# A Mamba scan's decay, states and sums in rings of their own, with one score tile fewer

## The chip, the cores and the metric

The kernel runs on one core of a Trainium2 chip. The metric is the device time of one execution, in microseconds (us), as the median of three runs. TensorE (PE in the profile, with its weight loads as PEld), VectorE (DVE), ScalarE (ACT), GpSimd (POOL) and SyncE (SP, which issues the DMAs) each work through a queue of their own in order. An instruction whose input is not ready holds up everything behind it on its engine.

## The reference

The model has two layers on eight batch rows of 64 latent tokens (width 512), which read a context of 1601 tokens per batch row. Everything is float32.

```
x = x + xattn0(layernorm(x), ctx)    # 32 query heads, 8 key/value heads of 128, over 1601 context rows
x = x + mamba(layernorm(x))          # d_in 1024, 16 states
x = x + ffn0(layernorm(x))           # ternary weight
x = x + xattn1(layernorm(x), ctx)    # softmax(x ctx^T) ctx
x = x + attn1(layernorm(x))          # causal, 32 heads
x = x + ffn1(layernorm(x))           # ternary octonion weights, gated
```

The part that the change touches is the recurrence inside `mamba`:

```
dA    = exp(dt_t * A)                          # decay, per channel and state
state = state * dA + (dt_t * u_t) * B_t        # over 64 time steps
y     = sum over the 16 states of state * C_t
```

after which `y + u * D` is gated and multiplied by the output matrix.

## The kernel before

The work is two programs that share the engines. The large one, `x_all`, is the first cross attention. It goes through 64 units, one for each batch row and key/value head. A unit has six steps. In these, PE projects keys (`x_k`, line 363) and values (`x_v`, line 334) from the context, makes scores of 13 blocks of 128 context rows (`x_s`, line 385), and multiplies the exponentials of the unit before by its values (`x_av`, line 464). ACT and DVE take the results out of PSUM: ACT copies values (line 337) and scores (line 388), and splits keys into a high and a low part with DVE (lines 108 and 109). DVE keeps the running maximum (lines 390, 392, 395), subtracts it (line 426) and normalises (lines 476, 477, 479). POOL sums the exponentials (lines 429, 446, 448, 452). Four PSUM buffers (`KVB = 4`) are shared by keys, values and scores.

The scores of a unit take seven tiles `S` of 128x512. They are written in one unit and read in the next, by the exponential, by POOL's sum and by PE's product with the values (`AVPLAN`: the product begins in the third step of the next unit). The ring of `S` holds `SB` tiles, 11 before the change. So the first four tiles of the new unit find a place at once, and each later one has to wait until a tile of the old unit has been read for the last time.

The second program is made of side chains: first a preparation of weights (`prep`), then for every pair of batch rows a `chain` of the other five blocks. While `x_all` runs, it reports a cost after each piece of its work, and `advance` lets each chain go forward as far as the constants `SPAN`, `CHAIN_COST` and `X_COST` say. The chains of the first three pairs run beside `x_all`; the chain of the fourth runs after it, with a path and buffers of its own (`tail`), together with what is left of the third. On DVE, ACT and POOL every instruction of a chain is pinned behind whatever was recorded before it on its engine (class `Late`). The instructions of `x_all` are not pinned: a scheduler that plays the program through on a model of the chip places them, and it may put later ones ahead of a pinned instruction that is not ready in its model. So the size of a ring changes the order of all the queues.

Beside `x_all`, `mamba` does its recurrence in 32 pieces per pair, eight blocks of 128 channels for each of four groups of four states (`scan`, line 895). A piece works on two tiles of 128x512, the decay `da` and the states `h`:

1. ACT: four exponentials into `da`; POOL: a memset of the first column of `da`, in some pieces `du = dt * u`, and then `h = B * du`.
2. DVE: the scan, which reads `da` and `h` and writes `h`.
3. `h * C`, on DVE in even pieces and on POOL in odd ones.
4. DVE: the sum over the states into `y`, and the addition to `u`.

`y` is the first quarter of `da`, so `da` is in use until the end of the piece. Both come from the ring `a2` of the pool for Mamba. One of its five tiles is held throughout by the transposed input of the block, which the gates after the scan still read, so four are left for the scan: two pieces. `a2` also serves the weights of the projections (`tw`: W_in, W_x and W_dt, loaded at lines 816, 844 and 869), the temporaries of `silu` and `softplus` (three at a time), the gate `z` and the split of the output (`mamba_out`). `B` and `C` come by a DMA (line 889) into `bc`, which has one buffer, once for each group of states: four times per pair.

Of the kernel before, what the change touches and what calls it, by code (L numbers as in the profile page):

```python
# [16 lines left out]
P = 128  # L17
D = 512
NC = 4
T = 64  # L20
# [16 lines left out]
PINNED = ("vector", "scalar", "gpsimd")  # L37
WOB = 3
KVB, OB, MB = 4, 1, 1
VB, SB = 16, 11  # L40
VPLAN = ((), (0,), (1, 2), (3,), (4, 5), (6,), (7,), (8,), (9, 10), (11,), (12,), ())
KPLAN = (1, 2, None, 3, None, 0)
CPLAN = (0, 1, 2, None, None, 3)
AVPLAN = ((), (), (0, 1, 2, 3), (4, 5, 6, 7), (8, 9, 10, 11), (12,))
EXPLAN = ((0,), (1, 2), (3,), (4, 5), (6,), ())
BUFS = {"a2": 5, "lv": 3, "bc": 1, "xpad": 1, "b2": 5, "b4": 2, "w2": 3, "xr": 2}
BUFS_TAIL = {"a2": 6, "du": 2, "bc": 2, "xpad": 4, "s4": 11, "kb": 3, "b2": 8, "b4": 3, "w2": 12, "xr": 2}


# [29 lines left out]
class Kernel:  # L79
# [13 lines left out]
    def sb(self, tag, shape, dt=FP, bufs=None, pool=None):  # L93
        if pool is None:
            pool, bufs = self.ca if tag in MAMBA_TAGS else self.cp, bufs or self.bufs.get(tag)
            if tag in REST and self.tp and not self.tail:
# [710 lines left out]
    def mamba(self, gi, x, xo):  # L807
# [40 lines left out]
        sm = self.sb("sm", [64, P], bufs=1)  # L848
# [36 lines left out]
        def bcast(sh):  # L885
            bc = self.sb("bc", [P, 2, HS, 2, T])
            for a in range(2):
                r = a * NST + sh * HS
                nc.sync.dma_start(
                    out=bc[:, a].rearrange("p s b t -> p (s b t)"),  # L890
                    in_=self.bc_s[gi][r : r + HS].rearrange("r t -> (r t)")[None, :].to_broadcast([P, HS * P]),
                )
            return bc

        def scan(c, sh, bc):
            da = self.sb(self.td, [P, HS, 2, T])
            for s in range(HS):
                k = sh * HS + s
                nc.scalar.activation(da[:, s], dt[:, c], AF.Exp, scale=self.A[:, c, k : k + 1])
            nc.gpsimd.memset(da[:, :, :, 0:1], 0.0)  # L900
            du = dus[:, c]
            if sh == 0:
                nc.gpsimd.tensor_tensor(du, dt[:, c], u[:, c], ALU.mult)
            h = self.sb(self.ts, [P, HS, 2, T])
            nc.gpsimd.tensor_tensor(h, bc[:, 0], du[:, None].to_broadcast([P, HS, 2, T]), ALU.mult)

            yield 1
            hf, df = h.rearrange("p s b t -> p (s b t)"), da.rearrange("p s b t -> p (s b t)")
            nc.vector.tensor_tensor_scan(hf, df, hf, 0.0, ALU.mult, ALU.add)
            yield 1  # L910
            (nc.gpsimd if c % 2 else nc.vector).tensor_tensor(h, h, bc[:, 1], ALU.mult)
            yield 1
            y = da[:, 0]
            nc.vector.tensor_reduce(y.rearrange("p b t -> p (b t)"), h.rearrange("p s b t -> p (b t) s"), AX.X, ALU.add)
            nc.vector.scalar_tensor_tensor(u[:, c], u[:, c], self.Dp[:, c : c + 1] if sh == 0 else 1.0, y, ALU.mult, ALU.add)
            yield 1

        wps = None
        if tail:
# [18 lines left out]
            for c in range(NCH):  # L938
                du = self.sb("du", [P, 2, T])
                nc.gpsimd.tensor_tensor(du, dt[:, c], u[:, c], ALU.mult)  # L940
                for k0 in range(0, NST, CS):
                    da = das[k0 // CS % 2]
                    for s in range(CS):
                        nc.scalar.activation(da[:, s, :, 1:], dt[:, c, :, 1:], AF.Exp, scale=self.A[:, c, k0 + s : k0 + s + 1])
                    bc, o = bcs[k0 // HS], k0 % HS
# [17 lines left out]
        else:  # L963
            for sh in range(nh):
                bc = bcast(sh)
                for c in range(NCH):
                    yield from scan(c, sh, bc)
# [332 lines left out]
    def run(self):  # L1300
        nc, tc, ctx = self.nc, self.tc, self.ctx
        nc.scalar.preload_act_table_set("natural_log_exp_and_others")
        self.setup(bufs=BUFS, accb=2, hs=4, tail=False, ahead=1, **TAGS)
        self.pc = ctx.enter_context(tc.tile_pool(name="pc", bufs=2, space=PSUM))
# [68 lines left out]
            advance(now)  # L1373


TAGS = {"tw": "a2", "ts": "a2", "td": "a2", "tc4": "b4", "tk": "b2", "t4": "w2", "tl": "b2", "tn": "w2", "tv": "lv"}
TAGS_TAIL = {"tw": "w2", "ts": "s4", "td": "s4", "tc4": "s4", "tk": "kb", "t4": "s4", "tl": "s4", "tn": "w2", "tv": "s4"}
ENV = ("nc", "cp", "ca", "pc", "bufs", "accb", "hs", "tail", "ahead", *TAGS)
GROUPS = {8: [2, 2, 2, 2], 2: [2]}
SPAN = [3.1,3.1,2.6,0.2]  # L1380
PREP_END = 2.8
MAMBA_TAGS = ("a2", "lv", "bc", "xpad", "sm")
FFN_TAIL = (("l", 0), ("l", 1), ("a", 0), ("l", 2), ("a", 1), ("d", 0), ("a", 2), ("d", 1), ("d", 2))
REST = {"w2":8,"b4":3}
OTB = 1
# [114 lines left out]
```

## Time and profile before

| | us |
|---|---|
| median of three runs | 2729.16 (2728.2 to 2729.43) |
| profiled execution, its own time | 2721.08 |
| its span | 2719.3 |
| PE busy | 2565.7 |
| DVE busy | 1746.8 |
| ACT busy | 1352.6 |
| POOL busy | 1171.4 |
| first to last scan, first pair | 768.5 to 1040.7 |
| first to last scan, second pair | 1411.3 to 1690.9 |
| first to last scan, third pair | 2033.3 to 2308.1 |

The span is from the first to the last instruction, 1.8 us less than the execution's own time. The profiled execution is 8.1 us shorter than the median of the runs. A row of the view by stretches gives a window, its length, and for each engine the busy time in it with the number of instructions, then the granted clock of PE as a share of full speed, the share of the DMA engines that were busy, and GB/s. In a row of the timeline the first number is the start, the second the duration, and the bracket at the end tells how long the engine had been idle and what ended that.

### The profile page before, as it was taken

What the parts mean: (1) busy time and instruction counts of PE and PEld (TensorE: products, weight loads), DVE (VectorE), ACT (ScalarE), POOL (GpSimd) and SP (SyncE); (2) the same over time, 40 slices, a digit from 0 to 9 for tenths busy, and PEclk for the clock granted to TensorE, in tenths of its full rate; (3) what the DMA queues carried; (4) which work ended last, traced back from release to release, by engine and by line L of the source; (5) the groups of instructions that cost most, each with busy time, mean ns of one, the idle gap of its engine ahead of it and who ended that gap; (6) DMA issues with size and microseconds to landing.
All of it is one profiled execution on the core that took longest, in us unless ns stands there. A gap on an engine that the chain in (4) does not pass through costs nothing.

```text
span 2719.3 us, 43920 instructions
## 1 busy us (share of the span) xinstructions
PE 2565.7 (94%) x16288; PEld 2273.7 (84%) x16288; DVE 1746.8 (64%) x2843; ACT 1352.6 (50%) x3128; POOL 1171.4 (43%) x1123
## 2 busy tenths in 40 slices
PE   7999999999998899999999988999999998986888
PEld 6999999889887899978988987997897898964644
DVE  4544345577688886545568689544668879457854
ACT  4444554445565554544455554544555455445543
POOL 3212434464588643422357346421249445114610
PEclk9999999999999999999999998999999999997999
DMA  9544446665665234665234443565342463476575
GB/s 308 153 141 153 138 144 228 200 204 178 214 218 188 75 121 159 211 184 174 88 109 134 152 136 106 185 206 186 116 133 80 128 187 113 148 256 201 195 264 188
DMA packets 302934, 455.59 MB, mean 168 GB/s; under 512 B 80248, under 2 KB 179576, under 8 KB 298240
## 3 DMA queue, kind: packets, MB, share of 16 engines
q1 hardware_dynamic: 302720, 452.79, 52.2%
q8 instruction: 128, 2.10, 0.3%
q14 instruction: 86, 0.70, 0.1%
HBM read 380.23 MB, written 72.48 MB: 166 GB/s over the span
## 4 chain that ended last, share of the span: by engine, by line
PE 47%; DVE 11%; DMA 4%; POOL 3%; issue 3%; ACT 2%; POOLq 0%; DVEq 0%; ACTq 0%; SPq 0%
PE v_ps L334 10%; PE k_ps L363 10%; PE o_ps L464 6%; PE s_ps L385 5%; DVE a L65 4%; PE w_ps L521 2%; PE acc L819 2%; PE acc L777 2%; PE acc L774 1%; PE acc L1092 1%; PE acc L1036 1%; POOL a L65 1%; POOL ss L452 1%; DVE acc L953 1%; PE acc L1178 1%
## 5 line engine op out<-in xcount | busy, mean ns | idle before, releaser
L363 PE MATMUL k_ps<-cxb,wk 128*128 128x384 f32 x2304 | 473.5, 348 | 36.4 <-DVE kt L109 12.6
L334 PE MATMUL v_ps<-wv,cxb 128*128 128x256 f32 x3456 | 474.1, 283 | 7.4 <-DVE mx L392 3.9
L334 PEld LDWEIGHTS v_ps<-wv,cxb 128*128 128x128 f32 x3456 | 441.8, 190 | 28.9 <-issue 13.6
L363 PEld LDWEIGHTS k_ps<-cxb,wk 128*128 128x128 f32 x2304 | 406.8, 192 | 56.3 <-DVE kt L109 14.3
L385 PE MATMUL s_ps<-q,kt 128*128 128x256 f32 (+1 forms) x2496 | 414.5, 299 | 8.6 <-DVE mx L392 7.2
L464 PE MATMUL o_ps<-S,v 128*128 128x256 f32 (+1 forms) x1664 | 413.6, 381 | 2.6 <-DVE rw L479 1.7
L388 ACT COPY S<-s_ps 128x512 f32<-128x512 f32 (+1 forms) x448 | 242.5, 554 | 252.6 <-PE s_ps L385 249.0
L385 PEld LDWEIGHTS s_ps<-q,kt 128*128 128x128 f32 (+1 forms) x2496 | 342.0, 185 | 30.3 <-DVE mx L392 8.5
L392 DVE TENSOR_TENSOR mx<-s_ps,mx 128x512 f32<-128x512 f32 x256 | 175.4, 685 | 297.5 <-ACT S L388 297.2
L452 POOL TENSOR_TENSOR ss<-ss,S 128x512 f32<-128x512 f32 x254 | 356.6, 1404 | 14.9 <-ACT S L427 0.3
L429 POOL TENSOR_TENSOR ss<-S,S 128x512 f32<-128x512 f32 x64 | 84.0, 1312 | 640.0 <-ACT S L427 639.9
L464 PEld LDWEIGHTS o_ps<-S,v 128*128 128x128 f32 (+1 forms) x1664 | 299.4, 190 | 41.6 <-issue 5.6
L426 DVE TENSOR_TENSOR S<-S,m_ps 128x512 f32<-128x512 f32 (+1 forms) x448 | 257.5, 641 | 36.2 <-PE m_ps L412 35.4
L108 ACT ACTIVATE kt<-k_ps,c_bk 128x384 fp32r<-128x384 f32 (+1 forms) x256 | 151.8, 593 | 246.2 <-PE k_ps L363 245.4
L427 ACT ACTIVATE S<-S 128x512 f32<-128x512 f32 (+1 forms) x448 | 247.6, 600 | 41.4 <-DVE S L426 41.0
L109 DVE SCALAR_TENSOR_TENSOR kt<-k_ps,c_bk,kt 128x384 fp32r<-128x384 f32 (+1 forms) x256 | 160.9, 629 | 156.2 <-ACT kt L108 155.0
L337 ACT COPY v<-v_ps 128x256 f32<-128x256 f32 (+1 forms) x416 | 152.1, 368 | 195.8 <-PE v_ps L334 192.7
L334 PE MATMUL v_ps<-wv,cxt 128*128 128x256 f32 (+1 forms) x1536 | 211.3, 286 | 5.1 <-DVE mx L392 5.1
L334 PEld LDWEIGHTS v_ps<-wv,cxt 128*128 128x128 f32 (+1 forms) x1536 | 194.6, 176 | 17.3 <-issue 5.9
L363 PE MATMUL k_ps<-cxt,wk 128*128 128x450 f32 x768 | 179.3, 376 | 0.0
L65 DVE TENSOR_TENSOR_SCAN a<-a,a 128x512 f32<-128x512 f32 x96 | 153.9, 1603 | 32.2 <-POOL a L65 32.0
L65 ACT ACTIVATE a<-lv,c_A_log 128x128 f32<-128x128 f32 x384 | 122.8, 392 | 85.8 <-DVE a L65 84.8
(358 smaller groups left out, 3951.3 us busy)
## 6 DMA issues: line engine op xcount, KB each, us to landing
wo<-d_wo SPq DMA_DIRECT2D x96, 512.0 KB, 5.6
wk<-d_wk SPq DMA_DIRECT2D x63, 512.0 KB, 4.3
wv<-d_wv SPq DMA_DIRECT2D x31, 1024.0 KB, 5.7
cst<-in_ctxT_dram SPq DMA_DIRECT2D x96, 192.0 KB, 2.7
b<-in_ctxN_dram SPq DMA_DIRECT2D x36, 512.0 KB, 3.8
d_q<-q_t SPq DMA_DIRECT2D x32, 512.0 KB, 4.3
q<-d_q SPq DMA_DIRECT2D x64, 256.0 KB, 3.0
d_wo<-b SPq DMA_DIRECT2D x32, 512.0 KB, 2.9
```

The costliest lines, as they stand in the source:

```text
L65: return lambda *a, **k: self.tc.keep_in_program_order(f(*a, **k))
L109: eng.scalar_tensor_tensor(lo, src, bias, hi.bitcast(FP), ALU.add, ALU.subtract)
L334: nc.tensor.matmul(ps[:r], lhsT=cx[:, a, c, o : o + r], rhs=w[:, m, c, :], start=k == 0, stop=k == 11)
L337: nc.scalar.copy(vt[:r], ps[:r])
L363: nc.tensor.matmul(ps[:, :wd], lhsT=w[:, a, c, :], rhs=cx[:, m, c, :], start=k == 0, stop=k == 11)
L385: nc.tensor.matmul(sp[:r, gi, :], lhsT=kt[:, a, o : o + r], rhs=q[:, m, :], start=k == 0, stop=k == 2)
L388: nc.scalar.copy(s[:r, :n], sp[:r, :n])
L392: nc.vector.tensor_tensor(mx, sp, S[0] if len(S) == 1 else mx, ALU.max)
L426: nc.vector.tensor_tensor(sv, sv, ps[:r, 1:2].to_broadcast([r, w, 256]), ALU.add)
L427: nc.scalar.activation(sv, sv, AF.Exp, scale=ISC)
L452: nc.gpsimd.tensor_tensor(ss, ss, S[n], ALU.add)
L464: nc.tensor.matmul(ps[:, 0], lhsT=self.v[(b, j, t)][:r, hc : hc + P], rhs=S[t // 2][:r, t % 2], start=t == 0, stop=t == NT - 1)
```

## The change

The decay `da` gets a ring `d` of two tiles, the sums `y` a ring of two small tiles (128x128) in place of a quarter of `da`, and the states share `a2`, which goes from five tiles to four. The scores `S` go from eleven tiles to ten. Per partition the decay takes 4 KB and the sums 1 KB, while `a2` and `S` give back 2 KB each. No instruction is added or removed. The path of the last pair (`BUFS_TAIL`, `TAGS_TAIL`) is as before.

```diff
-VB, SB = 16, 11
+VB, SB = 16, 10
...
-BUFS = {"a2": 5, "lv": 3, "bc": 1, "xpad": 1, "b2": 5, "b4": 2, "w2": 3, "xr": 2}
+BUFS = {"d": 2, "a2": 4, "y": 2, "lv": 3, "bc": 1, "xpad": 1, "b2": 5, "b4": 2, "w2": 3, "xr": 2}
...
-            y = da[:, 0]
+            y = self.sb("y", [P, 2, T])
             nc.vector.tensor_reduce(y.rearrange("p b t -> p (b t)"), h.rearrange("p s b t -> p (b t) s"), AX.X, ALU.add)
...
-TAGS = {"tw": "a2", "ts": "a2", "td": "a2", "tc4": "b4", "tk": "b2", "t4": "w2", "tl": "b2", "tn": "w2", "tv": "lv"}
+TAGS = {"tw": "a2", "ts": "a2", "td": "d", "tc4": "b4", "tk": "b2", "t4": "w2", "tl": "b2", "tn": "w2", "tv": "lv"}
...
-MAMBA_TAGS = ("a2", "lv", "bc", "xpad", "sm")
+MAMBA_TAGS = ("d", "a2", "y", "lv", "bc", "xpad", "sm")
```

## The prediction

> **What bounds the kernel now.** I read the page's engine totals first, then its groups, then the windows around the scans, then the timeline at single stalls.
>
> ```profile
> PE 2565.7 (94%) x16288; PEld 2273.7 (84%) x16288; DVE 1746.8 (64%) x2843; ACT 1352.6 (50%) x3128; POOL 1171.4 (43%) x1123
> ```
>
> PE is the bound, idle for 2719.3 - 2565.7 = 153.6 us. A change that leaves PE's work alone can only win or lose there. The next view cuts each of the three scan stages into four quarters of eight pieces, by the start of every eighth scan. The first number behind the length is PE's busy time, the third DVE's.
>
> ```profile
> core 0: us, PE busy (x) PEld busy (x) DVE busy (x) ACT busy (x) POOL busy (x), PEclk, DMA share, GB/s
> 768.50:844.70 76.20, 67.79 (x425) 63.93 (x425) 67.44 (x76) 42.67 (x101) 64.47 (x60) 0.93 0.67 224
> 844.70:921.70 77.00, 63.78 (x407) 60.24 (x405) 66.04 (x75) 45.68 (x115) 59.90 (x57) 0.96 0.42 124
> 921.70:984.60 62.90, 61.12 (x411) 58.75 (x411) 51.52 (x76) 33.83 (x83) 34.99 (x34) 1.00 0.31 94
> 984.60:1045.00 60.40, 60.40 (x398) 57.57 (x397) 50.11 (x74) 32.53 (x81) 33.67 (x32) 1.00 0.40 127
> 1411.30:1530.00 118.70, 115.07 (x796) 104.77 (x796) 91.90 (x136) 67.16 (x160) 78.58 (x74) 1.00 0.37 110
> 1530.00:1613.10 83.10, 82.74 (x527) 77.56 (x526) 61.29 (x90) 43.04 (x104) 34.64 (x38) 1.00 0.54 172
> 1613.10:1657.40 44.30, 36.94 (x215) 34.28 (x215) 40.07 (x53) 21.94 (x59) 25.54 (x29) 0.88 0.36 121
> 1657.40:1693.00 35.60, 26.73 (x151) 23.94 (x150) 34.88 (x45) 17.78 (x48) 18.46 (x19) 0.86 0.28 85
> 2033.30:2113.00 79.70, 76.70 (x524) 65.24 (x523) 70.43 (x96) 48.18 (x121) 71.80 (x70) 1.00 0.31 89
> 2113.00:2209.70 96.70, 92.27 (x572) 84.97 (x571) 71.92 (x106) 47.75 (x117) 42.97 (x44) 0.98 0.46 141
> 2209.70:2271.90 62.20, 59.79 (x384) 55.89 (x382) 51.38 (x79) 34.51 (x86) 32.61 (x32) 1.00 0.55 166
> 2271.90:2313.00 41.10, 35.04 (x216) 31.87 (x216) 38.18 (x53) 19.82 (x53) 24.33 (x25) 0.96 0.34 108
> ```
>
> PE's idle time is 8.4, 13.2, 1.8 and 0 us in the first pair, 3.6, 0.4, 7.4 and 8.9 in the second, 3.0, 4.4, 2.4 and 6.1 in the third: 59.6 us. It follows DVE's share. At 74 to 88% PE loses 0 to 4.4 us; in the three short quarters, at 90 to 98%, it loses 6 to 9. The first pair's two early quarters (88 and 86%) lose 8 and 13, since the preparation of weights loads POOL and DVE there too. Where PE idles, DVE sets the pace.
>
> ```profile
> L65 DVE TENSOR_TENSOR_SCAN a<-a,a 128x512 f32<-128x512 f32 x96 | 153.9, 1603 | 32.2 <-POOL a L65 32.0
> L65 ACT ACTIVATE a<-lv,c_A_log 128x128 f32<-128x128 f32 x384 | 122.8, 392 | 85.8 <-DVE a L65 84.8
> ```
>
> The ring shows here. ACT waits 84.8 us for DVE before exponentials (the decay waits for the sum of the piece two before it). But the scan's own 32.0 us of waiting is for POOL's `h`, much of it where `bc` had just been loaded.
>
> **The ring of decay and states.** Decay of piece c+2 now waits for scan c in place of its sum; `h` of piece c+2 no longer waits for the end of piece c. Nothing is added: 96 sums write another tile at the same 1068 ns. What does it free? This is the longest such wait but one:
>
> ```profile
> 1655.10 0.58 ACT L388 COPY S<-s_ps 128x512 f32<-128x512 f32 x1
> 1662.52 1.28 ACT L65 ACTIVATE a<-lv,c_A_log 128x128 f32<-128x128 f32 x4 [6.84 <-DVE a L65]
> 1663.70 0.56 ACT L108 ACTIVATE kt<-k_ps,c_bk 128x384 fp32r<-128x384 f32 x1
> ...
> 1657.36 2.34 DVE L65 TENSOR_TENSOR_SCAN a<-a,a 128x512 f32<-128x512 f32 x1 [3.22 <-POOL a L65]
> 1662.40 0.69 DVE L392 TENSOR_TENSOR mx<-s_ps,mx 128x512 f32<-128x512 f32 x1
> ```
>
> ACT is idle for 6.84 us with a key split behind it. PE then stands for 4.49 us, but it waits for the maximum at 1662.40, and DVE had worked without a break from 1657.36. Freed ACT finds the same DVE queue. Directly recoverable is the stall that ACT itself ends (scores after a copied value, 0.9 us) and part of PE's 4.5 us for the split output: I take -1, between 0 and -5.
>
> The Trainium skill (Perfetto Trace Analysis, Optimization Strategy) says that one gap repeating on the engine that should be saturated can mean too little memory for the next tile. Here it repeats on ACT, half idle; by the rule alone the ring would be worth up to the 84.8 us, by the row -1.
>
> Built, the change leaves more DVE work between an odd scan and its sum, which waits for POOL's product: at most two instructions stand there in 10 of 48 pieces, where it was 21. DVE waits 21.9 us for POOL before these sums. Half would go, and only DVE-bound quarters pass it on: -3, between 0 and -11.
>
> **Crowding.** The queue order of the built kernel shows how many of the cross attention's own DVE instructions stand in each quarter. Before: 47, 46, 48, 46; 76, 50, 24, 23; 45, 54, 43, 24. After: 62, 28, 48, 46; 68, 51, 23, 14; 46, 66, 28, 21. The side chain advances faster against the main work and clumps. Such a row takes DVE about 0.65 us (its maxima 0.685, splits 0.629, subtractions 0.641), and stands for 26.73 / 23 = 1.2 to 36.94 / 24 = 1.5 us of PE. In a DVE-bound quarter every row fewer thus adds 0.5 to 0.9 us of idle PE; I use 0.7. Second pair: 1 and 9 rows fewer, +7. Third pair: 3 rows, +2; and 43 to 28 goes four fifths of the way from a loss of 2.4 to one of 6.1, +3. First pair: the first quarter falls from 8.4 to the roomy quarters' 4, -4; the second loses 18 rows, +13, of which half, since it starts from 86% and PE can run ahead: +6. Roomy quarters: -1. Together +13. Four PSUM buffers let PE run some 4 x 1.5 us ahead at each clump, so I take half: +7, between 0 and +17 (all of it, and a third more).
>
> The clock is lower there too: 0.86 to 0.88 where PE idles most. The scan lasts 1.17 us at least but 1.60 on average, and 21 of the 96 last over 2.1, mostly 2.3, with a POOL product beside them. The Trainium skill (SBUF, Who interferes with whom) says DVE with two SBUF inputs and a reading POOL instruction exclude each other for the whole instruction. The trace agrees: 2.3 is about 1.2 plus a POOL product's 1.3. By the rule a denser stage could add 1.3 us to each of the 75 scans that are shorter than 2.1 us, up to 98 us of DVE; by the row the mean stays, and nothing is added here.
>
> **Ten score tiles.** From the score copies, POOL's sums and the value products I worked out when each tile is last read. With eleven the ring bites twice, 1.0 and 0.3 us:
>
> ```profile
> 806.41 0.59 ACT L388 COPY S<-s_ps 128x512 f32<-128x512 f32 x1 [0.99 <-PE o_ps L464]
> ```
>
> With ten at the same times, six of 448 copies would come too early, by 9.9, 5.6, 1.2, 0.8, 0.8 and 0.7 us, all in scan stages. Behind a waiting copy stand ACT's value and key evictions, so the PSUM buffers, so PE. The built order moves the value products of the worst unit ahead of its fourth score pair, which removes the 9.9. I take +3, between 0 and +19.
>
> **The narrower `a2`.** Three free tiles in place of four outside the scan. `softplus` takes three, so W_dt's second half loads only when one is given back; gates share two tiles for weights and `silu`. PE waited once for such a load (3.1 us; W_dt takes 2.6 to 5.3 to land). Three pairs: +3, between 0 and 3 x 4.0 = +12. SP's queue behind the load holds weights of the cross attention, ordered around it.
>
> **The tail.** In the built order two more of the third chain's eight score accumulations stand before the end of the main work. Each cost 4.5 to 5.8 us in the tail (3.4 to 4.7 of load, 1.1 of PE), and puts about 2 us of PE into the main part: -2, between -9 and +4.
>
> **Sum:** -1 - 3 + 7 + 3 + 3 - 2 = +7. The profiled execution's 2721.1 becomes 2728. It lies 8.1 below the median of the runs; on the median 2729.2 + 7 = 2736 us.
>
> **Rivals.** A: the ring was what held DVE and PE. For it: ACT's 84.8 us, and PE stalls next to blocked exponentials (4.7, 4.5, 1.9, 3.6, 2.4, 1.7, 0.9: 19.7 us). Against: DVE is unbroken in the two largest. If all these go and half my costs stay: 2729 - 20 + 6 = 2715. It decides once PE's idle time in the 12 quarters falls under 45 us. B: nothing reaches PE, whose other 94% is untouched: 2729 within 5.5 (0.2%, about what a measurement tells from no change). C: the score ring binds in every crowded quarter, because DVE's lateness delays the products: +19 for the ring, +17 for crowding, less 4: 2761. Against it is the moved product; for it the bite at 806.
>
> **How the numbers follow.** My forecast as slower by 0.2 to 0.8%: 0.38. C: 0.14. B: 0.2. A: 0.28. So slower 0.52, same 0.2, faster 0.28. The forecast's own range is 2735 to 2750. The wide one reaches into A and C, leaving out about 0.1 on each side: 2710 to 2756.
>
> **What would show it.** Right: exponentials' wait for DVE under 40 us; the second pair's last quarter shorter than 33 us with PE idle over 9; ACT score copies waiting for PE or POOL, some 5 us; PE's idle time over the three scan stages 62 to 75 us. Wrong: that idle time under 45 (A), or score copies waiting over 15 us (C). If main and side fall on the chip in another rhythm than the queue order suggests, the crowding term fails.

## The result, and the profile after

The changed kernel takes 2750.18 us (median of five runs, 2744.98 to 2754.3); before takes 2729.16 beside it (2723.94 to 2729.54). The ratio is 1.0088, 95% interval 1.0067 to 1.0108: slower by 18 to 29 us. The forecast was 2736, its own range 2735 to 2750, the wide range 2710 to 2756. So the direction was right, and the size was three times too small: 21 us where 7 were forecast, at the upper edge of its own range.

The profiled execution after has a span of 2747.9 us (its own time 2749.64, level with its median; that of before lay 8 us below its own). The engine totals of the page after:

```profile
PE 2570.4 (94%) x16288; PEld 2281.8 (83%) x16288; DVE 1738.4 (63%) x2843; ACT 1356.1 (49%) x3128; POOL 1164.3 (42%) x1123
```

PE is idle for 2747.9 - 2570.4 = 177.5 us (before 153.6) and busy for 4.7 us more with the same 16288 matmuls. So 23.9 of the 28.6 us between the two spans are idle PE. (The medians lie 21.0 apart.) The groups around the ring, by busy time, mean ns and idle time with its releaser:

```profile
L65 DVE TENSOR_TENSOR_SCAN a<-d,a 128x512 f32<-128x512 f32 x96 | 158.3, 1650 | 36.5 <-POOL a L65 36.5
L65 DVE TENSOR_REDUCE y<-a 128x128 f32<-128x512 f32 x96 | 102.1, 1068 | 17.0 <-POOL a L65 15.6 <-POOL d L65 0.8
L65 ACT ACTIVATE d<-lv,c_A_log 128x128 f32<-128x128 f32 x384 | 122.0, 392 | 99.6 <-DVE a L65 98.6 <-DVE lv L65 0.8
L388 ACT COPY S<-s_ps 128x512 f32<-128x512 f32 (+1 forms) x448 | 242.7, 553 | 267.3 <-PE s_ps L385 262.7 <-POOL ss L452 1.2 <-PE o_ps L464 0.8
```

The exponentials wait longer for DVE than before (98.6 us, it was 84.8), though their tile is free earlier: they wait for the scan now, and the scan is as late as its queue. The sums wait less for POOL's product (15.6, it was 21.9), the scans more (36.5, it was 32.0). Score copies wait for a POOL sum or a value product for 2.0 us in all.

The windows after, cut as before by every eighth scan; the last row is the tail, from the last value product to the end. The first number behind the length is PE's busy time, the third DVE's, and PEclk is the granted clock.

```profile
core 0: us, PE busy (x) PEld busy (x) DVE busy (x) ACT busy (x) POOL busy (x), PEclk, DMA share, GB/s
774.10:858.70 84.60, 73.55 (x484) 69.68 (x483) 73.62 (x91) 52.13 (x124) 73.20 (x70) 0.96 0.72 236
858.70:914.80 56.10, 46.98 (x273) 42.73 (x272) 46.80 (x57) 31.07 (x79) 48.40 (x44) 0.91 0.41 124
914.80:978.50 63.70, 63.70 (x432) 61.21 (x431) 52.27 (x76) 36.46 (x91) 34.81 (x35) 1.00 0.32 96
978.50:1038.70 60.20, 60.20 (x397) 57.40 (x396) 50.99 (x74) 32.45 (x81) 33.48 (x32) 1.00 0.40 127
1413.30:1525.10 111.80, 107.80 (x730) 97.20 (x730) 83.57 (x124) 60.63 (x145) 72.56 (x69) 0.98 0.39 113
1525.10:1611.60 86.50, 85.60 (x549) 80.13 (x548) 64.11 (x94) 44.51 (x108) 36.87 (x39) 1.00 0.55 169
1611.60:1654.60 43.00, 31.67 (x176) 28.83 (x175) 40.71 (x52) 20.76 (x56) 25.06 (x28) 0.84 0.33 108
1654.60:1684.80 30.20, 23.41 (x137) 21.54 (x137) 30.03 (x40) 14.74 (x42) 14.17 (x17) 0.89 0.19 54
2020.60:2097.00 76.40, 72.62 (x495) 60.83 (x494) 68.64 (x98) 44.86 (x114) 64.50 (x64) 1.00 0.30 87
2097.00:2192.90 95.90, 90.65 (x575) 84.90 (x576) 75.45 (x116) 52.13 (x123) 43.60 (x44) 0.98 0.44 132
2192.90:2252.80 59.90, 57.11 (x355) 52.88 (x353) 48.37 (x64) 28.55 (x74) 33.43 (x34) 0.97 0.53 167
2252.80:2294.10 41.30, 26.91 (x146) 24.16 (x147) 39.65 (x50) 18.54 (x50) 23.32 (x24) 0.83 0.21 72
2436.20:2747.90 311.70, 231.43 (x1275) 151.00 (x1274) 191.99 (x357) 136.73 (x361) 89.36 (x96) 0.87 0.64 210
```

The same window of before:

```profile
2412.80:2719.30 306.50, 240.40 (x1335) 153.55 (x1333) 192.31 (x364) 141.09 (x372) 89.55 (x96) 0.88 0.67 223
```

PE's idle time after is 11.0, 9.1, 0, 0 in the first pair, 4.0, 0.9, 11.3, 6.8 in the second, and 3.8, 5.3, 2.8, 14.4 in the third: 69.4 us (before 59.6). The second pair idles 2.8 us more and the first 3.2 less, which nearly cancel. The third went from 15.9 to 26.2, most of it in its last quarter (6.1 to 14.4). The tail idles for 311.7 - 231.4 = 80.3 us in place of 66.1. What lies outside scans and tail is the same within 0.1 us: 177.5 - 69.4 - 80.3 = 27.8 after, 153.6 - 59.6 - 66.1 = 27.9 before. So two places hold nearly all of the added idle time: the third pair's last quarter and the tail. The longest stall of each follows. The timeline after, at the last reload of `bc` of the third pair (start, duration; the bracket is the idle time before):

```profile
2247.20 0.80 SPq L889 DMA_DIRECT2D bc<-d_bc  x2
...
2251.54 2.50 POOL L65 TENSOR_TENSOR a<-bc,lv 128x512 f32<-128x512 f32 x2 [4.31 <-DMA bc<-d_bc]
...
2252.85 2.27 DVE L65 TENSOR_TENSOR_SCAN a<-d,a 128x512 f32<-128x512 f32 x1 [3.61 <-POOL a L65]
...
2255.15 1.28 ACT L65 ACTIVATE d<-lv,c_A_log 128x128 f32<-128x128 f32 x4 [7.42 <-DVE a L65]
...
2256.33 0.56 ACT L388 COPY S<-s_ps 128x512 f32<-128x512 f32 x1
...
2259.02 0.66 DVE L392 TENSOR_TENSOR mx<-s_ps,mx 128x512 f32<-128x512 f32 x1
...
2259.73 4.21 PE L363 MATMUL k_ps<-cxb,wk 128*128 128x384 f32 x12 [7.29 <-DVE mx L392]
```

POOL waits for `bc`, the scan for POOL, and the exponentials, now tied to the scan, for the scan: 7.42 us, with the score copy of the cross attention behind them on ACT. The maximum that frees PE's buffer comes 6 us later than the scan starts, and PE stands for 7.29 us. This stall and one of 5.02 us at 2276.95 (PE waits for DVE's reduced maximum) are 12.3 of the 14.4 us. At the same reload before, PE stood for 3.58. The tail, the longest stall after:

```profile
2493.84 1.56 PE L1036 MATMUL acc<-b,b 128*64 128x194 f32 x8 [6.92 <-DVE a L1008]
...
2496.41 1.26 DVE L65 TENSOR_REDUCE s1m<-b 64x1 f32<-64x512 f32 x2
...
2498.59 6.21 DVE L950 TENSOR_TENSOR s<-bc,du 128x512 f32<-128x512 f32 x4
...
2505.39 0.14 DVE L65 TENSOR_REDUCE s1m<-s1m 64x1 f32<-64x3 f32 x1
...
2505.56 0.72 ACT L65 ACTIVATE b<-b,s1m 64x512 f32<-64x512 f32 x1 [7.45 <-DVE s1m L65]
...
2506.43 1.40 PE L1074 MATMUL acc<-ident,b 64*128 64x64 f32 x8 [11.04 <-ACT b L65]
```

The third chain has made its last scores (of `xattn1`). Its softmax needs one maximum of 0.14 us from DVE, which stands behind four products of the fourth chain's scan (6.21 us), and PE has nothing else: 6.92 and 11.04 us of idle PE within 20 us. In before, 56 score matmuls of the third chain (line 1036; eight matmuls are one accumulation, so seven of them) lie beside the fourth chain's softplus and first products, from 2477 to 2500. After, seven of the 14 accumulations had already been made before the last value product.

But the longest stall is not where the tail loses most. These rows cut both tails at the fourth chain's first scan matmul (line 956) and at the last score matmul of all (line 1036), first before, then after:

```profile
2412.80:2495.10 82.30, 55.60 (x321) 35.61 (x319) 47.67 (x113) 36.34 (x107) 12.73 (x20) 0.77 0.81 270
2495.10:2609.70 114.60, 94.73 (x567) 66.61 (x567) 93.63 (x152) 64.17 (x180) 68.55 (x68) 0.88 0.60 198
2609.70:2719.30 109.60, 90.07 (x452) 51.33 (x448) 51.02 (x101) 40.57 (x88) 8.27 (x9) 0.97 0.62 214
```

```profile
2436.20:2508.70 72.50, 44.07 (x284) 30.03 (x283) 45.49 (x113) 34.64 (x103) 13.13 (x21) 0.82 0.87 291
2508.70:2627.60 118.90, 93.11 (x546) 66.66 (x547) 96.58 (x145) 61.98 (x174) 68.25 (x67) 0.87 0.55 177
2627.60:2747.90 120.30, 94.24 (x449) 54.31 (x444) 49.91 (x101) 40.12 (x87) 7.99 (x9) 0.90 0.58 195
```

Idle PE is 26.7, 19.9 and 19.5 us before, and 28.4, 25.8 and 26.1 after: 1.7, 5.9 and 6.5 more. The first stretch, with the stall above, idles hardly more than before, where PE waits 11.6 us in the tail for the loads of the third chain's scores; with fewer matmuls it is 9.8 us shorter. The last stretch has no score matmul left and, but for four transposes, the same matmuls as before. It takes 10.7 us longer: 6.5 us of idle time, and 4.2 us of busy time at a granted clock of 0.90 in place of 0.97.

### The profile page after: what moved, and what is told of

Its sections match the earlier page's. It is cut to its first block, busy times and chain, and to the rows that moved or that the text cites. A ratio compares the mean times of both kernels' runs of the same rounds, so it can differ in the third digit from the quotient of the medians.

```text
span 2747.9 us, 43977 instructions
## 1 busy us (share of the span) xinstructions
PE 2570.4 (94%) x16288; PEld 2281.8 (83%) x16288; DVE 1738.4 (63%) x2843; ACT 1356.1 (49%) x3128; POOL 1164.3 (42%) x1123
## 4 chain that ended last, share of the span: by engine, by line
PE 46%; DVE 14%; POOL 4%; DMA 3%; issue 3%; ACT 2%; SPq 0%; POOLq 0%; DVEq 0%; ACTq 0%
PE v_ps L334 10%; PE k_ps L363 10%; PE o_ps L464 7%; PE s_ps L385 5%; DVE a L65 4%; PE w_ps L521 2%; PE acc L1036 2%; PE acc L819 2%; DVE y L65 2%; PE acc L1092 2%; PE acc L774 2%; PE acc L777 1%; DVE S L426 1%; POOL a L65 1%; DVE acc L953 1%
## 5 line engine op out<-in xcount | busy, mean ns | idle before, releaser
L65 DVE TENSOR_TENSOR_SCAN a<-d,a 128x512 f32<-128x512 f32 x96 | 158.3, 1650 | 36.5 <-POOL a L65 36.5
L65 ACT ACTIVATE d<-lv,c_A_log 128x128 f32<-128x128 f32 x384 | 122.0, 392 | 99.6 <-DVE a L65 98.6
```

The lines of the kernel that those rows point to most:

```text
L65: return lambda *a, **k: self.tc.keep_in_program_order(f(*a, **k))
```

## The experiments

Three notes for what follows. "Record" in an expectation means the terms of the prediction, and "trace" what the two profiles made likely in their place. A run's time is given as its ratio to before's runs on the same chip. The expectations count the tail's idle PE to the last matmul (63 us before, 77 after); the windows run to the end of the span, which is three us more (66 and 80).

**Ten score tiles alone.**

```diff
 # before
-VB, SB = 16, 11
+VB, SB = 16, 10
```

> The kernel before with ten score tiles and nothing else; its queues differ from before's only within one unit of the first pair. Record (the prediction's term): +3 us, between 0 and +19, that is 2732, with score copies that wait for a value product or a POOL sum, about 5 us in all. Trace (read from the two profiles): in the kernel after, score copies wait for value products for 0.8 us in all, so the ten tiles cost nothing: 2729 within 4 us.

Measured: 2728.69 against 2728.53 us, ratio 0.9995 (0.9981 to 1.0008). The score copies' group:

```profile
L388 ACT COPY S<-s_ps 128x512 f32<-128x512 f32 (+1 forms) x448 | 242.2, 553 | 252.8 <-PE s_ps L385 248.7 <-POOL lv L65 0.7 <-POOL a L65 0.6
```

No sum and no value product is among the three largest releasers. Ten tiles cost nothing that can be told from zero: between -5 and +2 us.

**Four tiles in `a2` alone.**

```diff
 # before
-BUFS = {"a2": 5,
+BUFS = {"a2": 4,
```

> The kernel before with four tiles in a2 in place of five: the scan then has three tiles for a decay and its states, and softplus and the gates have one less. It bounds the narrower a2 from above, since the scan is narrower here too. Record: +3, between 0 and +12, from W_dt and the gates, and the scan on top. Its queues keep all 14 of the third chain's score accumulations behind the last value product, as before, and its third pair has 56, 58, 40 and 33 rows of cross attention in its quarters (before 45, 54, 43, 24). Trace: where no row is lost in the last quarter and the tail keeps its 14 accumulations, nothing of the 21 us is lost: 2729 within 5, unless the narrower scan itself holds DVE, which would show as more than 10 us of idle PE per pair.

Measured: ratio 1.0049 (1.0032 to 1.0065). That is 9 to 18 us, mostly above the record's upper end of 12, and not the trace reading's "2729 within 5" either: both missed. Outside scans and tail PE idles 27.3 us (before 27.9), and in the scans 52.8 (before 59.6). The loss shows in a tail of 340.5 us that idles 85.3: the third chain runs late, the last value product comes 17 us earlier than before, and more is left for the end (1367 matmuls in the tail, before 1335). What delays the chain:

```profile
L65 ACT ACTIVATE a<-lv,c_A_log 128x128 f32<-128x128 f32 x384 | 122.7, 391 | 132.3 <-DVE lv L65 132.1 <-DVE a L65 0.2
```

With three tiles for the scan the exponentials wait for the end of a piece, 132 us in all, and that does not reach PE inside the scans. So no cost of softplus and the gates shows for the lost tile, and what the slower scan costs appears in the tail.

**The sums alone in a tile of their own.**

```diff
 # before
-BUFS = {"a2": 5,
+BUFS = {"a2": 5, "y": 2,
...
-            y = da[:, 0]
+            y = self.sb("y", [P, 2, T])
...
-MAMBA_TAGS = ("a2",
+MAMBA_TAGS = ("a2", "y",
```

> The kernel before with the sums alone in a tile of their own (1 KB): the decay is free after the scan, a2 keeps five tiles and the scores eleven. Built, the first two pairs have the rows of before, the third 48, 64, 33, 18 (before 45, 54, 43, 24), and seven of the third chain's 14 score accumulations stand before the last value product, as in the kernel after (before none). Record: ring -4, crowding in the third pair +2 and +4, tail -2: 0, so 2729 within 5. Trace: the tail loses the work that covers its waits, about +14 of idle PE less some work done earlier, and the last quarter of the third pair idles 10 to 15 us (before 6.1): +10 to +22, so 2739 to 2751.

Measured: ratio 1.0054 (1.0034 to 1.0074), 2744. Third pair idle 22.2 us (before 15.9), tail 83.5 (before 66.1), first two pairs 39.3 (before 43.6). Time and tail are as the trace reading expected, the last quarter is not: it idles 7.0 us, where 10 to 15 were expected, and the third pair loses in its second and third quarters. So freeing the decay early, without any other ring touched, already costs more than half of what the change costs, in the tail and the third pair, though not in the same quarter.

**Another pace, no ring touched.** The constant `SPAN` tells in how much progress of the cross attention a chain has to be done.

```diff
 # before
-SPAN = [3.1,3.1,2.6,0.2]
+SPAN = [3.1,3.1,2.66,0.2]
```

> The kernel before with all its rings, but the third chain a little slower (SPAN 2.66 for 2.6). Queues differ only from the third pair on: 46, 70, 34, 22 rows in its quarters, and seven of the 14 score accumulations before the last value product. No ring is changed. Record: two quarters a little poorer, +3, and the tail -2: 2730 within 4. Trace: if the tail's lost cover is what costs, it is lost here too: +8 to +18 with the tail's idle PE near 80 us (before 66, after 80), so 2737 to 2747, with no change of any ring.

Measured: ratio 1.0046 (1.003 to 1.0063). Third pair 24.7, tail 74.7. An order like that of the changed kernel from the third pair on costs 0.46% with before's rings.

**The changed kernel at pace 2.58.**

```diff
 # after
-SPAN = [3.1,3.1,2.6,0.2]
+SPAN = [3.1,3.1,2.58,0.2]
```

> The kernel after with all its rings, but the third chain's pace 2.58 for 2.6. Its first two pairs have the queues of the kernel after; the third pair has 46, 70, 48, 20 rows (after 46, 66, 28, 21), and all 14 score accumulations of the third chain are behind the last value product, as in the kernel before (after seven). Pace theory (third pair and tail lose, for want of the same order): tail idle back from 77 us to between 60 and 68, third pair idle 18 to 24 (after 26): 10 to 17 us less than after, 2733 to 2740. Ring theory (what is lost comes from the rings and the first two pairs' queues, which are those of after): 2750 within 4. Record: fuller third quarter -3, tail +2: 2749.

Measured: ratio 1.0029 (1.0015 to 1.0042). Two thirds of the loss are gone, with every ring and the queues of the first two pairs as in the kernel after. Last two quarters of the third pair, and the tail:

```profile
2203.00:2275.60 72.60, 69.72 (x449) 64.74 (x449) 56.80 (x85) 36.77 (x92) 32.07 (x35) 1.00 0.50 161
2275.60:2309.30 33.70, 28.92 (x170) 26.75 (x170) 33.55 (x46) 18.51 (x50) 19.47 (x20) 0.90 0.20 63
2412.30:2727.70 315.40, 243.12 (x1335) 156.64 (x1333) 189.56 (x364) 140.80 (x372) 87.30 (x96) 0.86 0.65 217
```

The last quarter idles 4.8 us (after 14.4), the tail 72.3 (after 80.3). The ring theory (2750 within 4) falls; the third pair came out better than the pace theory expected (14.5 against 18 to 24), the tail at the upper end (69 as the expectation counts, against 60 to 68). And the last stretch of its tail, after the last score matmul, is 119.8 us long with no score early (after 120.3, before 109.6).

**Scores early, late quarters as before; and the reverse.** Both with before's rings.

```diff
 # before, first run
-SPAN = [3.1,3.1,2.6,0.2]
+SPAN = [3.1,3.1,2.54,0.2]
 # before, second run
-SPAN = [3.1,3.1,2.6,0.2]
+SPAN = [3.1,3.1,2.58,0.2]
```

> The kernel before with all its rings, third chain's pace 2.54. Rows of the third pair 38, 60, 45, 24 (before 45, 54, 43, 24), so its two late quarters are those of before; but seven of the 14 score accumulations stand before the last value product, as in the kernel after. Tail theory: idle PE in the tail 71 to 82 us (before 63), third pair 14 to 18 (before 16): +5 to +12, 2734 to 2741. If the quarters of the third pair are the cost and the tail is not: 2729 within 4. Record's tail term: -2 to -4 for seven accumulations done early, 2726.

> The kernel before with all its rings, third chain's pace 2.58. Rows of the third pair 45, 73, 46, 17 (before 45, 54, 43, 24); all 14 score accumulations behind the last value product, as before. Crowding theory: idle PE in the last quarter 10 to 15 us (before 6.1), third pair 20 to 26 (before 16), tail 61 to 66: +4 to +10, 2733 to 2739. Tail theory alone: 2729 within 4. Record: seven rows fewer in the last quarter at 0.7 us, +5, halved +2.5: 2731.

Measured: scores early 1.0017 (1.0002 to 1.0031), with the third pair at 16.5 and the tail at 72.1 (69 as the expectation counts): of the sign that the tail theory asked for, and just under its size. The last stretch of its tail is 110.1 us long, as in before, with seven early. The reverse 0.9976 (0.996 to 0.9993): faster than before. Its last two quarters:

```profile
2236.10:2301.90 65.80, 65.64 (x426) 61.61 (x426) 57.07 (x82) 35.05 (x89) 27.72 (x30) 1.00 0.53 160
2301.90:2337.10 35.20, 29.33 (x176) 26.70 (x175) 33.59 (x44) 16.20 (x45) 26.81 (x24) 0.95 0.33 107
```

The last quarter has seven rows fewer than before and idles 5.9 us, where 10 to 15 were expected. A quarter's own count is no measure: the two late quarters count together (below).

**Sums apart at pace 2.58.**

```diff
 # the kernel with the sums apart
-SPAN = [3.1,3.1,2.6,0.2]
+SPAN = [3.1,3.1,2.58,0.2]
```

> The kernel with the sums apart (sixteen-tile and eleven-tile rings as before), third chain's pace 2.58. First two pairs' rows as before, third pair 49, 64, 47, 22, and two of the 14 score accumulations before the last value product (seven in the run with the sums apart at pace 2.6). Pace theory: tail idle 62 to 70 us (80.6 there), third pair 16 to 20 (22 there): 10 to 17 us less than there, 2727 to 2734, level with before: then sums apart neither gain nor lose. Ring theory (the freed decay gains 4 us in its own right): 2725. If the sums' own tile costs by itself: 2744 within 4.

Measured: ratio 1.0036 (1.0022 to 1.0049), 2737 us beside 2725. On the scale of the expectation that is 2739, which misses the pace theory (2727 to 2734) and the ring theory (2725) and lies nearest the third, 2744 within 4: only two accumulations are early, and still the tail idles 78.1 us (about 75 as the expectation counts, where 62 to 70 were expected). Against before's rings at the same pace, the sums apart cost 0.54% at 2.6 and 0.60% at 2.58 (the quotients of the ratios), at 2.58 as much as all the rings. Whether their tile or the order that came with it costs that is not shown.

**The changed kernel at two more paces.**

```diff
 # after, two runs
-SPAN = [3.1,3.1,2.6,0.2]
+SPAN = [3.1,3.1,2.54,0.2]
...
+SPAN = [3.1,3.1,2.66,0.2]
```

> The kernel after with all its rings, third chain's pace 2.54: the partner of the run with before's rings at that pace, which took 0.17% more than before. Third pair 46, 67, 44, 24 rows, seven of the 14 score accumulations before the last value product. At pace 2.6 the change costs +0.88%, at 2.58 it costs 1.0029 against 0.9976, +0.53%. Order theory (the loss is how the third pair and the tail happen to fall): at this pace the change costs anything between -0.3% and +0.8%, with the idle PE of pairs one and two as in the kernel after (20 and 23 us). Cost theory (the rings lose of themselves): again +0.5 to +0.9%, 2742 to 2755.

> The kernel after with all its rings, third chain's pace 2.66: the partner of the run with before's rings at that pace, which took 0.46% more than before. Third pair 51, 67, 44, 22 rows, seven accumulations before the last value product. Order theory: the change costs between -0.4% and +0.6% here (2727 to 2755). Cost theory: +0.5 to +0.9% on top of 2740, 2754 to 2765.

Measured: 1.0067 (1.0043 to 1.0092) and 1.0036 (1.0024 to 1.0049). The change by pace, as the quotient of the two ratios: +0.50% at 2.54, +0.53% at 2.58, +0.88% at 2.6, -0.10% at 2.66 (each within about 0.3). The first fits both theories; the last refutes that the rings cost 0.5% of themselves at every pace.

**Only the tail's order.**

```diff
 # after, and before
-SPAN = [3.1,3.1,2.6,0.2]
+SPAN = [3.1,3.1,2.6,0.25]
```

> The kernel after, the fourth chain's pace 0.25 for 0.2. Every queue is that of the kernel after up to the tail (PE's first 3377 of 3749 rows); only the order of the third and fourth chains' work in the tail differs, and no ring, no buffer and no amount of work. Tail-order theory: the idle PE of the tail (77 us in after, 63 in before, 63 to 82 in the others) moves by 5 to 14 us, and the time with it, by preference down: 2736 to 2745. If the tail's idle time follows from what was left over for it (seven accumulations fewer): 2750 within 4.

> The kernel before, the fourth chain's pace 0.25 for 0.2. Queues as before up to the tail (PE's first 3362 of 3747 rows), rings as before. Tail-order theory: before has the lowest idle PE in the tail of all runs (63 us), so another order loses: 68 to 78 us, +5 to +14, 2731 to 2740. If the tail's idle time follows from what was left over for it: 2726 within 4.

Measured: 1.0096 (1.0075 to 1.0117) and 0.999 (0.9975 to 1.0006). The tails, first after, then before, each with the new pace of the fourth chain:

```profile
2437.10:2752.60 315.50, 233.79 (x1275) 150.57 (x1274) 192.79 (x354) 136.52 (x361) 89.22 (x96) 0.86 0.62 208
2411.50:2719.30 307.80, 241.97 (x1334) 155.08 (x1333) 192.52 (x364) 141.34 (x372) 89.55 (x96) 0.88 0.66 222
```

The theory that the tail's order decides finds support on neither side: the tail idles 81.7 and 65.8 us, as in after (80.3) and before (66.1). This other interleaving of the two chains changed nothing in either kernel, so the difference between the two tails does not come from this pace. By time, the second run meets the other reading (2726 within 4), and the first lies at the upper end of its 2750 within 4 or above it (2750 to 2761). The two runs are also second profiles of the same queues up to the tail: the last quarter of the third pair idles 13.4 and 6.1 us, as in the first profiles (14.4 and 6.1; its two stalls again, 7.22 and 4.61 us), so that difference is no scatter of single executions.

**What all traces say together.** Late rows are the cross attention's own DVE instructions in the two late quarters, in the built queues; late idle is PE's idle time there; early is how many of the third chain's 14 score accumulations stand before the last value product.

| kernel | pace | ratio | late rows, third pair | late idle, third pair | early | tail idle |
|---|---|---|---|---|---|---|
| before | 2.6 | 1 | 67 | 8.5 | 0 | 66.1 |
| before, 10 scores | 2.6 | 0.9995 | 67 | 8.4 | 0 | 66.5 |
| before, fourth at 0.25 | 2.6 | 0.999 | 67 | 8.8 | 0 | 65.8 |
| before | 2.58 | 0.9976 | 63 | 6.1 | 0 | 66.5 |
| before | 2.54 | 1.0017 | 69 | 8.2 | 7 | 72.1 |
| before | 2.66 | 1.0046 | 56 | 13.1 | 7 | 74.7 |
| sums apart | 2.6 | 1.0054 | 51 | 12.2 | 7 | 83.5 |
| sums apart | 2.58 | 1.0036 | 69 | 11.4 | 2 | 78.1 |
| after | 2.6 | 1.0088 | 49 | 17.1 | 7 | 80.3 |
| after, fourth at 0.25 | 2.6 | 1.0096 | 49 | 17.5 | 7 | 81.7 |
| after | 2.58 | 1.0029 | 68 | 7.7 | 0 | 72.3 |
| after | 2.54 | 1.0067 | 68 | 11.4 | 7 | 80.7 |
| after | 2.66 | 1.0036 | 66 | 14.9 | 7 | 70.6 |

With the second pair's late quarters (46 or 47 rows and 15 to 18 us without the change's rings, 37 rows and 18 to 20 us with them) and both pairs of the narrow `a2`, these are 28 points. A straight line through them is 30.8 us less 0.31 us per row (correlation -0.90, the farthest point 5.0 us off). The second pair's points repeat a few orders; the third pair's 14 alone give about the same slope and a correlation of only -0.72. So a row that leaves the two late quarters goes with some 0.31 us of idle PE. It is a line through whole kernels: no run moved rows and nothing else.

## Why the prediction was right, and where it was not

**Direction and scan stages.** Crowding was the forecast's largest term, and idle PE in the scans rose as it said: 62 to 75 us were forecast over the three stages, 69.4 were measured, against 59.6. That fewer rows are the cause fits the line through all traces; no run isolates it. That the time moved the way it was forecast owes something to luck: the same change at pace 2.66 measured -0.10%. Rival A needed under 45, and rival B an unchanged PE: both are out.

**Crowding, +7.** The second pair was put at +7, halved; it measured +2.8 for ten rows fewer (and 4.2 between the means of the five profiles with all rings and the six with before's). The third was put at +5, halved, and measured +10.3 (18 rows fewer in the two late quarters; the line gives 5.6). The first was put at +2, halved, and measured -3.2 (-4.3 between the means). The price of 0.7 us per row was more than twice the 0.31 of the runs, so the halving was right as a number, by luck; the reason given for it, the four PSUM buffers, was not tested. The step that failed is the third pair's last quarter, priced by its own three rows at +2: it cost 8.3. A quarter with 21 rows after one with 28 is worse than one with 17 after one with 46 (14.4 and 5.9 us). And the timeline has a stall that the sum did not have: the exponentials, waiting for a scan that waits for `bc`, with a score copy behind them. That a third decay tile would remove it is argued from the timeline; it was not tried.

**The tail, -2.** This sign was wrong. The step said that score accumulations done early take load time out of the tail and put only their PE time into the main part, and it counted two of eight. Seven of 14 were early, and the tail has 60 matmuls fewer, but it became 5.2 us longer. It is the largest single miss, +14.2 us of idle PE. The step itself nearly holds where it looked: the stretch up to the fourth chain's first scan matmul became 9.8 us shorter. But the waits for loads that went were replaced there by waits for the fourth chain's softplus and first products on DVE, which the scores had covered, so its idle time stayed (26.7 and 28.4 us). What the step put at nothing is the rest of the tail: 12.4 us more idle time behind that, 6.5 of them behind the last score matmul. With before's rings early scores cost 6 to 9 us of idle tail, net of the work moved 0.17% in the run whose third pair was as before. The early scores are only a part of it, though: with seven early the tail idles 14 to 17 us more at 2.6 with the sums apart or all rings, and 14.6 at 2.54, but 4.5 with all rings at 2.66, and with none or two early the tails at 2.58 with all rings or the sums apart still idle 6 and 12 us more than before's. The last stretch takes 120 us with none early (all rings, 2.58) and 110 with seven (before's rings, 2.54), so it does not go by them. What makes it long is open; the two runs at 0.25 show only that it is not the pace of the fourth chain.

**Ten score tiles, +3: nothing.** Measured alone -5 to +2 us, and 2.0 us of waiting copies in the kernel after, where some 5 were forecast. Rival C (2761, copies waiting over 15 us) had the time nearer than the forecast, and its mechanism is out.

**Narrower `a2`, +3: nothing** outside the scans (27.8 us of idle PE in the kernel after and 27.3 with four tiles alone, before 27.9).

**Ring, -1 and -3.** Exponentials were to wait for DVE under 40 us; they wait 98.6. The forecast had itself argued that freed ACT finds the same DVE queue, and then gave a sign to look for that followed from the opposite. The Trainium skill (Perfetto Trace Analysis, Optimization Strategy) connects a gap repeating on the saturated engine with too little memory for the next tile. Here the gap was on ACT; more memory left it at 98.6 us, and between 82.5 and 97.3 in the four other runs with all rings, where before's rings show 84.1 to 100.0 in six profiles; and the time rose. DVE's waits for POOL before sums were to fall by half of 21.9 us; they fell by 6.3, and those before scans rose by 4.5. The order moves them as much: 14.8 us with before's rings at 2.58, 24.2 with all rings at 2.54. In the first two pairs, where the rings and their queues are the same in all runs with them, PE idles 42.6 to 45.2 us, and 41.5 to 48.6 with before's rings: no gain and no loss.

**The second pair's last quarter** was to be shorter than 33 us with more than 9 us idle: 30.2, and 6.8.

**What the sum did not have: PE's own time.** The same matmuls take 2569.4 to 2572.3 us in the five profiles with all rings of the change, and 2563.1 to 2569.7 in the six with before's (one of them with ten score tiles). In the third pair's last quarter the granted clock is 0.83 and 0.79 in the two profiles after; with before's queues it is 0.96 in two, and 0.92 in the run with ten score tiles. The 12 key matmuls behind the 7.29 us stall take 4.21 us, 12 of the same form after it, at 2266.28, take 2.37. The Trainium skill (TensorE: Matmul & The Clock Gate, What's actually happening) says that after a window of about 3.4 us without work the clock is halved, until about as long a stretch of work; the stalls of 7.29 and 5.02 us in this quarter agree with it: the trace grants half the clock from 2257.3 to 2264.1 and from 2274.3 to 2281.1. The kernel after at pace 2.58 has no stall over 2.1 us there and still shows 0.90, since its stalls of 1.90 and 2.08 us have only 0.56 us of work between them; the clock is halved from 2284.9 to 2291.7. So a stretch that is idle for the most part was enough. The term is worth 3 to 5 us over the whole run, and the tail's last stretch alone is busy for 4.2 us longer.

Together at pace 2.6, from the means of two profiles after and three of before (those with the fourth chain at 0.25 and the ten score tiles among them): third pair +11.2, tail +14.9, PE's own time +3.3, first two pairs +0.3, the rest -1.6: 28.1 us between the mean spans, where the timed runs say 18 to 29. The mechanism of the forecast is thus right in part: its sum has crowding in the third pair, too small, the tail with the wrong sign, and PE's own time not at all. How much of the loss belongs to the rings and how much to the order that came with them: at four paces the change costs +0.50, +0.53, +0.88 and -0.10% (0.45% on average), and the pace alone, without any ring, moves the time by -0.24 to +0.46%. A benefit of the rings shows at none of them.

## What to carry to other kernels

A ring size in a kernel whose queues are placed by a scheduler is also a draw of another order: before its effect is judged, build neighbours that change only the order (a pace constant), and compare at several. A wait is worth removing only where the engine that ends it is not itself the queue that everybody waits for; here ACT's 85 us were DVE's lateness, seen from ACT. And the longest stall is not yet the loss: cut both kernels at the same piece of work and compare the stretches. The tail's longest stall lay in a stretch that idled 1.7 us more than before, and the other 12.4 us came behind it.

## What was not expected of the hardware

A quarter in which PE idles longer cost it twice, by the idle time and by a lower granted clock: 0.83 with 14.4 us idle in 41.3, 0.96 with 6.1 in 41.1. A scan took 1650 ns on average in place of 1603, although POOL's products and the tiles are of the same size; at pace 2.58 with the same rings it took 1591, and over all orders 1591 to 1650 with all rings and 1563 to 1611 with before's. The Trainium skill (SBUF — State Buffer, Who interferes with whom) has DVE and POOL exclude each other when DVE reads two inputs from SBUF and POOL reads there too; the estimate of up to 98 us that the prediction worked out from it did not come. The measured shift is 96 x 47 ns = 4.5 us, or -1.2 at the other pace.
